# A two-layer convolution kernel: the 3x3 weights transformed in other rooms, their taps loaded first, image 0 on two queues, and new costs in the planner

## The chip, the core and the metric

The kernel runs on one core of a Trainium2 chip. Five engines matter here. TensorE (PE in the profile) multiplies matrices, and its weight loads have a row of their own (PEld). VectorE (DVE) and ScalarE (ACT) do elementwise work. GpSimd (POOL) and SyncE (SP) mostly issue transfers; ScalarE can issue them too. Each engine runs its own instructions strictly in the order of the program and waits for the others on semaphores. All transfers run on the core's 16 DMA engines, whatever engine issued them. The metric is the time of one execution on the device in microseconds. Three runs of the kernel before gave 2394.2, 2396.96 and 2401.03 us; the median, 2396.96 us, is the time before. The profiled execution spans 2394.4 us.

## The reference

Sixteen images of 1024 channels and 32x32 pixels, all float32, pass through two residual layers. Cut to what matters (`bn` is a scale and a shift per channel, `unfold3x3` gives the nine shifted copies of a map):

```python
# layer 0: bottleneck with 3x3 local self-attention, 32 heads of 8 channels
h    = relu(bn(conv1x1(x, w_conv1)))                # 1024 -> 256
q, k = relu(bn(conv1x1(h, wq))), relu(bn(conv1x1(h, wk)))
v    = bn(conv1x1(h, wv))
attn = softmax(einsum('bgdhw,bgdkhw->bgkhw', q, unfold3x3(k) + pos))   # over 9 taps
out  = einsum('bgdkhw,bgkhw->bgdhw', unfold3x3(v), attn)
x    = relu(bn(conv1x1(relu(bn(out)), w_conv3)) + x)                   # 256 -> 1024
# layer 1: bottleneck with an ordinary 3x3 convolution
h    = relu(bn(conv1x1(x, w1)))                     # 1024 -> 256
h    = relu(bn(conv3x3(h, w2)))
x    = relu(bn(conv1x1(h, w3)) + x)                 # 256 -> 1024
```

## The kernel before

The work is a hand-written list of stages per image. P is the first convolution of layer 0 (C) followed by the projections to k and q (Q) and to v (V). F is layer 0's last convolution fused with layer 1's first. W is the 3x3 convolution of four images at once, in Winograd form. U is layer 1's last convolution. The list begins `P0 P1 P2 P3 F0 P4 F1 ...` and ends `F12 F13 F14 U10:0123 F15 U10:4567 U11:01234 W12 U11:567 U12 U13 U14 U15`. TensorE walks it in this order.

VectorE does the attention (`logits`, `weighted`) and the Winograd transforms (`transform`, and `along`, `middle`, `last` in `winograd_conv`). ScalarE empties TensorE's accumulators (results, k, q, v, `by_offset`), seeds them with the residual input (L396), applies the exponentials (L642) and the relu of a finished attention (L704). Because each engine is in order, the place of every VectorE and ScalarE instruction among the others is fixed when the program is built. That is the task of class `Side`: a planner with two clocks of estimates, `tensor` and `vector`. A stage adds its cost to `tensor`; a job on VectorE yields the estimated cost of its next part, which is added to `vector`; a part is put into the program when its time on the `vector` clock comes within 4 us of `tensor`. An attention job starts no sooner than `RELAY` = 13 us after its operands were sent, and its exponentials are put into ScalarE's program when the `tensor` clock gets near the time planned for them. The estimates take no part when the kernel runs; they only set the order.

Before the first image the kernel must prepare weights. `load_taps` fetches the 3x3 weights (the taps, six transfers of 384 KB), `winograd_weights` transforms them: for each of two halves m, `sums` makes five rows along one axis, and `along` makes six rows (i) of the result from these, each 768 KB, which SyncE stores to DRAM as `uw` (L291, 12 stores). `sums` is three or four ScalarE and six VectorE instructions. Each row is built in a tile of pool `hpool` (5 buffers, shared with h, q and the attended maps), so a row can't begin before an earlier store has left its buffer. `load_scaled`, `scale_rows` and `scale_weights` scale two more weights and store them as `ws`. The planner runs both as `side.first` jobs from time 24 on. Pool `apool` holds the attention's operands under the tags qc, bnk, bnv, pc and e; at the start they are empty, except that the taps lie in e and bnv.

Attention of an image takes its q, k, v and position terms back from DRAM in another layout: they are stored (`q<-q`, `bnk<-kp`, `pos<-by_offset`) and loaded again (L575, `qc`, `bnk`, `pc`, `bnv`), which `relay` issues on GpSimd.

Transfers of image 0's input go out on ScalarE's queue, those of the others on GpSimd's (L345). `Side.held` and `release` hold the exponentials of image 0 back until the first convolution of image 2 has been emptied (L1066).

Of the kernel before, what the change touches and what calls it, by code (L numbers as in the profile page):

```python
# [72 lines left out]
def sa_bottleneck_kernel(ctx: ExitStack, tc: tile.TileContext, x, w1t, wqkvt, w3t, u1t, u2t, u3t, params, out):  # L73
# [92 lines left out]


    members = const.tile([P, G], F32, tag="members", name="members")
    nc.gpsimd.memset(members, 1.0)
    for base, sign in ((0, 1), (HEAD_DIM - 1, -1)):  # L170
        nc.gpsimd.affine_select(
            out=members,
            in_=members,
            compare_op=ALU.is_ge,
            fill=0.0,
            base=base,
            pattern=[[-sign * HEAD_DIM, G]],
            channel_multiplier=sign,
        )

# [20 lines left out]


    kp = const.tile([P, NW, H + 2, PW], F32, tag="kp", name="kp")
    nc.gpsimd.memset(kp, 0.0)
    vh = const.tile([P, NW * VROWS, VW], F32, tag="vh", name="vh")


# [23 lines left out]
    def scale_weights():  # L233

        for which in range(2):

            scale = scales[which].rearrange("p (m o) -> p o m", o=NC)
            shape = [P, NW, NC // 2, P]
            for half in range(2):
                t = scaled[which, half].rearrange("p n (o m) -> p n o m", m=P)  # L240
                nc.vector.tensor_tensor(
                    t, t, scale[:, half * NC // 2 :][:, : NC // 2].unsqueeze(1).to_broadcast(shape), ALU.mult
                )
                nc.sync.dma_start(ws[which, half], scaled[which, half])
                yield 1.3
# [14 lines left out]

    def winograd_weights():

        n = 3 * WID
        first, second = (ppool.tile([P, 4 * HW], F32, tag="t", name="g") for _ in range(2))
        one, two, three = first[:, : 2 * HW], first[:, 2 * HW :], second[:, : 2 * HW]

        def sums(dst, a, s, t0, t1):

            nc.scalar.activation(t0, a[1], AF.Identity, scale=-1 / 6)
            nc.scalar.activation(t1, a[1], AF.Identity, scale=1 / 12)  # L270
            nc.vector.tensor_add(s, a[0], a[2])
# [5 lines left out]
            nc.scalar.activation(dst[0], a[0], AF.Identity, scale=0.25)  # L277
            if dst[5] is not None:
                nc.scalar.activation(dst[5], a[2], AF.Identity)

        def along(m, i, row):

            t = hpool.tile([P, 2 * HW], F32, tag="h", name="u")[:, : NI * WID]
            u = t.rearrange("p (j o) -> p j o", j=NI)
            small = three[:, 2 * n :].rearrange("p (j o) -> p j o", o=WID)
            sums(
                [u[:, COLUMNS.index(j)] for j in range(NI)],
                [row[:, j * WID : (j + 1) * WID] for j in range(3)],
                small[:, 0], small[:, 1], one[:, 2 * n : 2 * n + WID],
            )  # L290
            nc.sync.dma_start(uw[i, :, :, m].rearrange("k p j o -> p k (j o)"), t.rearrange("p (k n) -> p k n", k=3))  # L291

        for m, g in enumerate(taps):
            rows_ = [one[:, :n], one[:, n : 2 * n], two[:, :n], two[:, n : 2 * n], three[:, :n]]

            s, t = three[:, n : 2 * n], second[:, 2 * HW :]
            sums(rows_ + [None], g, s, t[:, :n], t[:, n : 2 * n])
            yield 6.0
            for i, row in enumerate(rows_ + [g[2]]):
                along(m, i, row)  # L300
                yield 3.0

    def inside(t, n):
        return t[:, n, 1 : 1 + H, 1 : 1 + W]
# [10 lines left out]
    def more_loads():  # L315

        while loads and live[0] < CHUNKS + RESULTS - 1:
# [24 lines left out]
                t = xpool.tile([P, NK * 2 * PART], F32, tag="x", name=name)  # L342
                t = t if kind == "V" else t[:, :HW]

            (nc.scalar if kind == "x" and b == 0 else nc.gpsimd).dma_start(t, src)  # L345
            loaded[loads.pop(0)] = t
            live[0] += 1

# [110 lines left out]
    def project(b):  # L459
# [84 lines left out]
        side.add(b)  # L544
        written.add(("qk", b))
        relay("qk", b)
        yield 2.5
# [46 lines left out]
    def logits(b):  # L594
# [4 lines left out]
        for k in range(0, KK, 2):  # L599
            of = min(2, KK - k)  # L600
            for two in range(of):
                i, j = divmod(k + two, 3)
                nc.vector.tensor_tensor(  # L603
                    by_row(t[:, two]), by_row(qc), kc[:, :, i : i + JROWS, j : j + W], ALU.mult
                )
            yield 2.3 * of
            u = t[:, :of]
            nc.vector.tensor_add(u[:, :, 0:4], u[:, :, 0:4], u[:, :, 4:8])  # L608
            nc.vector.tensor_add(u[:, :, 0:2], u[:, :, 0:2], u[:, :, 2:4])
            nc.vector.tensor_add(e[:, k : k + of, :], u[:, :, 0], u[:, :, 1])  # L610
            yield 2.3 * of
# [8 lines left out]
        yield 3.5  # L620

        def tree(op, to):
            t = zpool.tile([P, 4, JPIX], F32, tag="z", name="tree")
# [100 lines left out]
    def transform(b, src):  # L724
# [28 lines left out]
        d = [AP(src.tensor, src.offset + i * VW, [src.ap[0], [4 * VW, LINES], [1, VW]]) for i in range(NI)]  # L753
        for make, two in pairs:
            make([t[:, i] for i in two], d)
            yield 3.4

        room = form_room(b)
        t = t.rearrange("p i l w -> p (i l) w")
        for make, two in pairs:  # L760
            v = [zpool.tile([P, HW], F32, tag="z", name="v")[:, : NI * PART] for _ in two]
            make([u.rearrange("p (l c) -> p l c", c=TR) for u in v], [t[:, :, at : at + TR] for at in PLACES])
            for j, u in zip(two, v):
                at = COLUMNS.index(j)
                nc.sync.dma_start(
                    room[:, at // 2, :, b % NK, at % 2].rearrange("i p e -> p i e"),
                    u.rearrange("p (i e) -> p i e", i=NI),
                )
            if two != (1, 2):
                key = b - b % NK, two == (0, 5)  # L770
                forms[key] = forms.get(key, 0) + 1
                more_loads()

            yield 4.3, 0.0 if b % NK == NK - 1 else 3.0

    def winograd_conv(b):

# [69 lines left out]
        def last(i):  # L847
# [11 lines left out]
            if i == 4:  # L859
# [4 lines left out]
                return 11.0  # L864
# [5 lines left out]
        for one, two in ROWS:  # L870
            for part in range(3):
                for i in (one, two):
# [3 lines left out]
                    elif part == 1:  # L876
                        copied(i, twos, 1.0)
                        side.other(along(i))
                        if i == 0:

                            middle(3, 0, 4.0)
                            side.other(6.0)
                    else:
                        side.other(last(i))
                    yield CHUNK + 0.3

    hidden_one = {}

# [8 lines left out]
    class Side:  # L897
# [3 lines left out]
        def __init__(self):  # L901
            self.tensor = self.vector = 8.0
            self.jobs, self.firsts, self.exp, self.ready = [], [], None, {}
            self.held = False

        def add(self, b):

# [6 lines left out]
        def begins(self):  # L914

            other, at = None, 1e6
            if self.jobs:
# [1 line left out]
                what = other["needs"], other["b"]  # L919
                at = max(self.vector, other["at"], come[what] + RELAY if what in come else 1e6)  # L920
                if self.exp:
                    at = 1e6 if self.held else max(at, self.exp[0] + EXP)
            if self.firsts:
                job = self.firsts[0]
                ready = max(self.vector, job["at"])
# [3 lines left out]

        def step(self):  # L930
            job, self.vector = self.begins()
            if self.exp and not self.held and ("needs" in job or self.exp[0] < self.tensor):
                self.fire()
            cost = next(job["parts"], "end")
            if cost == "end":
# [7 lines left out]
                job["needs"] = cost  # L943
            elif callable(cost):
                self.exp = self.vector - 0.0, cost
                if job["b"] == 0:

                    self.held = True
            else:
                self.vector += cost  # L950

# [3 lines left out]
            self.exp = None  # L955
            self.jobs[0]["at"] = max(at, self.tensor) + EXP

        def release(self):

            if self.held:  # L960
                self.held, at = False, self.exp[0]
                self.fire()
                self.jobs[0]["at"] = at + EXP

        def run(self):
            while True:
                if self.exp and not self.held and self.exp[0] < self.tensor + 4.0:
# [89 lines left out]
    def first_conv(b):  # L1057

        ps = two_sums()
        for c in range(NC):  # L1060
            reduce_part(c, ps, loaded.pop(("x", b, c)), "w1")
            free()
            if c == NC - 1:
                h = hidden[b] = hpool.tile([P, NW, HW], F32, tag="h", name=f"h_{b}")
                for n in range(NW):
                    nc.scalar.activation(  # L1066
                        h[:, n, :], ps[n], RELU, bias=col("L0_conv_bn1_b", n), scale=col("L0_conv_bn1_s", n)
                    )
# [358 lines left out]
```

## Time and profile before

| | value | where from |
|---|---|---|
| time, median of 3 | 2396.96 us | the times |
| span of the profiled execution | 2394.4 us | the page |
| PE busy | 2357.5 us, 98% | page, part 1 |
| DVE busy | 2163.4 us, 90% | page, part 1 |
| ACT busy | 933.2 us, 39% | page, part 1 |
| moved in the first 100 us | 370 GB/s, DMA share 1.00 | the table of windows |
| moved over the span | 289 GB/s | page, part 2 |

PE's busy share counts pipelined instructions, so 98% doesn't mean 98% of its peak; what it does say is that PE has only some 37 us without an instruction. The list of PE's waits tells what ended each of them. In the timeline a row gives the start, the length, the engine, the line, the operation, what it writes and reads, and in brackets the idle time ahead of it and what ended that. A row can stand for several instructions of the same kind (x8). For DMA issues the row tells when the queue's instruction ran, and the DMA view from when to when the bytes moved.

### The profile page before, as it was taken

The numbers are of one execution on the slowest core, as the hardware profiler recorded it, in microseconds if no ns is written. First come the engines' busy times: TensorE is split into PE (matmuls) and PEld (weight loads), VectorE is DVE, ScalarE is ACT, GpSimd is POOL, SyncE is SP. The second block draws the span as 40 slices with busy tenths as digits, with TensorE's granted clock in tenths as the row PEclk, the third lists the DMA queues.
The fourth block names the chain that finished last, engine by engine and source line by source line (L and its number), as shares of the span: only waits on it lengthen the run. The fifth ranks groups of instructions, "written<-read, shape, count | busy, mean of one in ns | idle before, by whom it ended". The sixth has DMA issues, their size and how long they took to land. (4 is left out here: it accounts for less than half of the span.)

```text
span 2394.4 us, 18854 instructions
## 1 busy us (share of the span) xinstructions
PE 2357.5 (98%) x6240; PEld 1141.1 (48%) x6240; DVE 2163.4 (90%) x1783; ACT 933.2 (39%) x891; POOL 490.8 (20%) x901
## 2 busy tenths in 40 slices
PE   8999999999999999999999999999999999999998
PEld 3443444444466444444466444444466444434843
DVE  4899999999999999998999999989989999874687
ACT  3324142323122574443122574334222553344278
POOL 3212121212121231111111232111111221111222
PEclk9999999999999999999999999999999999999999
DMA  9968696878797898676898997787798986787877
GB/s 362 362 215 307 251 301 211 276 284 265 273 341 264 318 393 301 233 266 227 250 315 293 302 404 294 240 283 276 239 323 299 316 332 224 252 281 266 328 285 293
DMA packets 296769, 691.08 MB, mean 289 GB/s; under 512 B 20832, under 2 KB 167264, under 8 KB 288224
## 3 DMA queue, kind: packets, MB, share of 16 engines
q0 software_dynamic: 119648, 470.88, 54.1%
q1 hardware_dynamic: 175648, 214.49, 27.9%
q10 hardware_dynamic: 1376, 4.51, 0.5%
q8 instruction: 50, 0.82, 0.1%
q14 instruction: 47, 0.39, 0.0%
HBM read 416.09 MB, written 273.70 MB: 288 GB/s over the span
## 5 line engine op out<-in xcount | busy, mean ns | idle before, releaser
L405 PE MATMUL ps<-a,w 128*128 128x512 f32 x1024 | 461.8, 596 | 6.6 <-ACT a L704 5.5
L373 PE MATMUL ps<-result,u 128*128 128x512 f32 x1024 | 457.8, 592 | 0.0
L373 PE MATMUL ps<-x,w 128*128 128x512 f32 x1024 | 444.4, 595 | 6.8 <-DMA x<-in_x_dram 6.8
L660 DVE TENSOR_TENSOR acc<-e,bnv 128x2048 f32<-128x2048 f32 x144 | 327.6, 2284 | 31.7 <-ACT e L642 28.6
L405 PE MATMUL ps<-y,u 128*128 128x512 f32 x768 | 331.3, 592 | 1.2 <-ACT ps L396 1.2
L603 DVE TENSOR_TENSOR prod<-qc,bnk 128x2048 f32<-128x2048 f32 x144 | 324.1, 2287 | 1.7
L432 ACT ACTIVATE result<-ps,par 128x1024 f32<-128x1024 f32 x128 | 142.5, 1113 | 457.9 <-PE ps L405 389.1
L405 PEld LDWEIGHTS ps<-a,w 128*128 128x128 f32 x1024 | 195.5, 191 | 255.2 <-issue 243.9
L373 PEld LDWEIGHTS ps<-x,w 128*128 128x128 f32 x1024 | 195.3, 191 | 252.5 <-issue 252.3
L373 PEld LDWEIGHTS ps<-result,u 128*128 128x128 f32 x1024 | 194.4, 190 | 245.1 <-issue 237.7
L678 DVE TENSOR_TENSOR acc<-acc 128x2048 f32<-128x2048 f32 x128 | 293.4, 2292 | 4.4
L405 PEld LDWEIGHTS ps<-y,u 128*128 128x128 f32 x768 | 145.8, 190 | 184.8 <-issue 180.8
L469 PE MATMUL ps<-h,wqk 128*128 128x512 f32 x512 | 222.3, 592 | 0.0
L433 POOL DMA_DIRECT2D r<-result x128 | 68.7, 537 | 632.1 <-ACT result L432 626.6
L608 DVE TENSOR_TENSOR prod<-prod 128x2048 f32<-128x2048 f32 (+1 forms) x80 | 166.2, 2078 | 2.5
L469 PEld LDWEIGHTS ps<-h,wqk 128*128 128x128 f32 x512 | 97.2, 190 | 122.6 <-issue 110.0
L1066 ACT ACTIVATE h<-ps,par 128x1024 f32<-128x1024 f32 x32 | 38.5, 1204 | 284.2 <-PE ps L373 284.2
L432 ACT ACTIVATE result<-ps,bn_sh 128x1024 f32<-128x1024 f32 x96 | 106.6, 1111 | 100.2 <-PE ps L405 98.4
L481 ACT ACTIVATE kp<-ps,par 128x1024 f32<-128x1024 f32 x64 | 77.4, 1210 | 154.9 <-PE ps L469 113.1
L396 ACT ACTIVATE ps<-s 128x1024 f32<-128x1024 f32 x128 | 131.2, 1025 | 2.5
L345 POOL DMA_DIRECT2D x<-in_x_dram x120 | 63.7, 532 | 291.3 <-PE ps L373 222.5
L469 PE MATMUL ps<-h,wv 128*128 128x512 f32 x256 | 117.0, 610 | 4.2 <-ACT by_offset L522 4.2
(376 smaller groups left out, 2618.1 us busy)
## 6 DMA issues: line engine op xcount, KB each, us to landing
s<-in_x_dram POOLq DMA_DIRECT2D x128, 512.0 KB, 6.2
r<-result POOLq DMA_DIRECT2D x128, 512.0 KB, 3.8
out_dram<-result POOLq DMA_DIRECT2D x126, 512.0 KB, 6.5
x<-in_x_dram POOLq DMA_DIRECT2D x120, 512.0 KB, 5.0
r<-r POOLq DMA_DIRECT2D x111, 512.0 KB, 7.2
v<-v SPq DMA_DIRECT2D x96, 408.0 KB, 4.5
U<-uw SPq DMA_DIRECT2D x72, 512.0 KB, 4.8
bnk<-kp SPq DMA_DIRECT2D x32, 680.0 KB, 7.0
```

What stands on the lines that cost most here:

```text
L345: (nc.scalar if kind == "x" and b == 0 else nc.gpsimd).dma_start(t, src)
L373: nc.tensor.matmul(ps[n][:, halves(half)], wt[:, c % (NC // 2), n * P : (n + 1) * P], src[:, halves(half)], start=(c == first), stop=(c == ...
L396: nc.scalar.activation(ps, loaded.pop((self.kind, self.b, o)), AF.Identity)
L405: nc.tensor.matmul(self.ahead[o][:, halves(half)], pieces[key][:, n, o % (NC // 2) * P :][:, :P], self.src[:, n, halves(half)], start=Fals ...
L432: nc.scalar.activation(to_, ps, RELU, bias=self.shift(o), scale=1.0)
L433: nc.gpsimd.dma_start(to, t)
L469: nc.tensor.matmul(ps[:, halves(half)], pieces[key][:, m, at : at + P], h[:, m, halves(half)], start=(m == 0), stop=(m == NW - 1),)
L481: nc.scalar.activation(dst, src, func, bias=col(f"L0_conv_{name}_b", n), scale=col(f"L0_conv_{name}_s", n),)
L603: nc.vector.tensor_tensor(by_row(t[:, two]), by_row(qc), kc[:, :, i : i + JROWS, j : j + W], ALU.mult)
L608: nc.vector.tensor_add(u[:, :, 0:4], u[:, :, 0:4], u[:, :, 4:8])
L660: nc.vector.tensor_tensor(by_row(dst), rows(e[:, k, :]).unsqueeze(1).to_broadcast([P, HEAD_DIM, JROWS, W]), vc[:, :, i : i + JROWS, j : j ...
L678: nc.vector.tensor_add(acc, acc, t)
```

## The change

It has four parts.

1. **Rooms.** A row of the transformed 3x3 weights is no longer built in `hpool` alone, but in tiles that the attention doesn't use yet (qc, bnk, e), in a free quarter of `second` (`four`), or in `hpool`. ScalarE's share of a row (`parts_of`) is split from VectorE's (`sums`) and is put one row ahead (`begin` before `finish`), with its own pair of scratch columns.
2. **Taps first, two queues.** The taps of the first half go out ahead of everything else on GpSimd, those of the second right after; the helper mask and the clearing of `kp` follow. Of image 0's eight input pieces four stay on ScalarE's queue and four go to SyncE's. The two loads for the scaled weights move to the third and fourth step of image 0.
3. **Costs.** The numbers that jobs yield to the planner are replaced by measured ones, and the two jobs of weights start at 15 instead of 24.
4. **No hold.** `held` and `release` go: image 0's exponentials are planned as the others' are.

All of it moves work; the arithmetic is the same.

```diff
@@ at_first
     def at_first():
+        load_taps(0)
+        more_weights()
         more_weights()
         more_loads()
+        load_taps(1)
+        head_members()
+        nc.gpsimd.memset(kp, 0.0)
         norms()
-        for m in range(NW):
-            load_taps(m)
-        load_scaled()
-        scale_rows()
-        for _ in range(3):
+        for _ in range(2):
             more_weights()
         position_table()
-        side.first(winograd_weights(), 24.0, 0.0)
-        side.first(scale_weights(), 24.0, 0.0)
+        side.first(winograd_weights(), 15.0, 0.0)
+        side.first(scale_weights(), 15.0, 0.0)
+        hooks["conv1", 0, 2] = load_scaled
+        hooks["conv1", 0, 3] = scale_rows
@@ winograd_weights
+        def room(where):
+
+            if where == "h":
+                t = hpool.tile([P, 2 * HW], F32, tag="h", name="u")
+            elif where == "four":
+                t = four
+            else:
+                shape = {"e": [P, KK, JPIX], "qc": [P, HEAD_DIM, JPIX], "bnk": [P, HEAD_DIM, HALO]}[where]
+                t = apool.tile(shape, F32, tag=where, name="u").rearrange("p a b -> p (a b)")
+            return t[:, : NI * WID]
+
+        rooms = (("qc", "bnk", "four", "h", "qc", "bnk"), ("h", "e", "qc", "four", "bnk", "e"))
...
-            for i, row in enumerate(rows_ + [g[2]]):
-                along(m, i, row)
-                yield 3.0
+            begun = begin(m, 0, rows_[0])
+            for i in range(NI):
+                following = begin(m, i + 1, (rows_ + [g[2]])[i + 1]) if i + 1 < NI else None
+                finish(m, i, *begun)
+                begun = following
+                yield 2.6
@@ more_loads
-            (nc.scalar if kind == "x" and b == 0 else nc.gpsimd).dma_start(t, src)
+            engine = nc.gpsimd
+            if kind == "x" and b == 0:
+                engine = nc.scalar if c < NC // 2 else nc.sync
+            engine.dma_start(t, src)
@@ logits
             nc.vector.tensor_add(e[:, k : k + of, :], u[:, :, 0], u[:, :, 1])
-            yield 2.3 * of
+            yield 4.24 if of == 2 else 2.36
@@ transform
             make([t[:, i] for i in two], d)
-            yield 3.4
+            yield 3.2
...
-            yield 4.3, 0.0 if b % NK == NK - 1 else 3.0
+            yield 4.05, 0.0 if b % NK == NK - 1 else 3.0
@@ Side
-                    at = 1e6 if self.held else max(at, self.exp[0] + EXP)
+                    at = max(at, self.exp[0] + EXP)
...
-                if job["b"] == 0:
-
-                    self.held = True
@@ first_conv
-                if b == 2:
-                    side.release()
```

Smaller costs change too: 2.3 to 2.29 per product in `logits`, 3.5 to 3.55 for the position terms, 2.5 to 1.1 after the positions in `project`, 1.3 to 2.0 in `scale_weights`, 11.0 to 11.4 and 6.0 to 5.5 in the 3x3 convolution, and its step of CHUNK + 0.3 becomes CHUNK (3.43).

More of the change, by code (lines that the diff above doesn't have):

```diff
@@ L168, in sa_bottleneck_kernel, with head_members @@
     members = const.tile([P, G], F32, tag="members", name="members")
[L169 to L179, printed above, removed]
+    def head_members():
+        nc.gpsimd.memset(members, 1.0)
+        for base, sign in ((0, 1), (HEAD_DIM - 1, -1)):
+            nc.gpsimd.affine_select(
+                out=members,
+                in_=members,
+                compare_op=ALU.is_ge,
+                fill=0.0,
+                base=base,
+                pattern=[[-sign * HEAD_DIM, G]],
+                channel_multiplier=sign,
+            )
     offsets = const.tile([P, NW, NPOS], F32, tag="offsets", name="offsets")
@@ L205, in sa_bottleneck_kernel @@
     kp = const.tile([P, NW, H + 2, PW], F32, tag="kp", name="kp")
-    nc.gpsimd.memset(kp, 0.0)
     vh = const.tile([P, NW * VROWS, VW], F32, tag="vh", name="vh")
@@ L244, in scale_weights @@
                 nc.sync.dma_start(ws[which, half], scaled[which, half])
-                yield 1.3
+                yield 2.0
     taps = []
@@ L264, in winograd_weights, with parts_of, sums @@
         first, second = (ppool.tile([P, 4 * HW], F32, tag="t", name="g") for _ in range(2))
-        one, two, three = first[:, : 2 * HW], first[:, 2 * HW :], second[:, : 2 * HW]
-        def sums(dst, a, s, t0, t1):
+        one, two, three, four = first[:, : 2 * HW], first[:, 2 * HW :], second[:, : 2 * HW], second[:, 2 * HW :]
+        def parts_of(a, t0, t1, to0, to5):
             nc.scalar.activation(t0, a[1], AF.Identity, scale=-1 / 6)
             nc.scalar.activation(t1, a[1], AF.Identity, scale=1 / 12)
+            nc.scalar.activation(to0, a[0], AF.Identity, scale=0.25)
+            if to5 is not None:
+                nc.scalar.activation(to5, a[2], AF.Identity)
+        def sums(dst, a, s, t0, t1):
             nc.vector.tensor_add(s, a[0], a[2])
@@ L276, in sums, with begin, finish @@
                 nc.vector.scalar_tensor_tensor(to, s, 1 / 6, t1, ALU.mult, op)
[L277 to L283, printed above, removed]
-            u = t.rearrange("p (j o) -> p j o", j=NI)
[L285 to L290, printed above, removed]
+        def room(where):
[8 more added lines that the diff above has]
+        rooms = (("qc", "bnk", "four", "h", "qc", "bnk"), ("h", "e", "qc", "four", "bnk", "e"))
+        small = [t[:, 2 * n :].rearrange("p (j o) -> p j o", o=WID) for t in (one, two, three)]
+        def begin(m, i, row):
+            t = room(rooms[m][i])
+            u = t.rearrange("p (j o) -> p j o", j=NI)
+            dst = [u[:, COLUMNS.index(j)] for j in range(NI)]
+            a = [row[:, j * WID : (j + 1) * WID] for j in range(3)]
+            t0, t1 = small[i % 2][:, 0], small[i % 2][:, 1]
+            parts_of(a, t0, t1, dst[0], dst[5])
+            return t, dst, a, t0, t1
+        def finish(m, i, t, dst, a, t0, t1):
+            sums(dst, a, small[2][:, 0], t0, t1)
             nc.sync.dma_start(uw[i, :, :, m].rearrange("k p j o -> p k (j o)"), t.rearrange("p (k n) -> p k n", k=3))
@@ L294, in winograd_weights @@
             rows_ = [one[:, :n], one[:, n : 2 * n], two[:, :n], two[:, n : 2 * n], three[:, :n]]
-            s, t = three[:, n : 2 * n], second[:, 2 * HW :]
-            sums(rows_ + [None], g, s, t[:, :n], t[:, n : 2 * n])
+            parts_of(g, four[:, :n], four[:, n : 2 * n], rows_[0], None)
+            sums(rows_ + [None], g, three[:, n : 2 * n], four[:, :n], four[:, n : 2 * n])
             yield 6.0
-            for i, row in enumerate(rows_ + [g[2]]):
-                along(m, i, row)
-                yield 3.0
+            begun = begin(m, 0, rows_[0])
[4 more added lines that the diff above has]
+                yield 2.6
     def inside(t, n):
@@ L546, in project @@
         relay("qk", b)
-        yield 2.5
+        yield 1.1
         for n, cost in enumerate(halo("bnv", 2, AF.Identity)):
@@ L605, in logits @@
                 )
-            yield 2.3 * of
+            yield 2.29 * of
             u = t[:, :of]
@@ L610, in logits @@
             nc.vector.tensor_add(e[:, k : k + of, :], u[:, :, 0], u[:, :, 1])
-            yield 2.3 * of
+            yield 4.24 if of == 2 else 2.36
         pc = projected[b]["pos"]
@@ L619, in logits @@
         nc.vector.tensor_tensor(part, part, pc[:, 2:4].unsqueeze(1).to_broadcast(shape), ALU.add)
-        yield 3.5
+        yield 3.55
         def tree(op, to):
@@ L863, in last @@
                 middle(4, 1, 8.0)
-                return 11.0
+                return 11.4
             r = 0 if i == 0 else 3
@@ L881, in winograd_conv @@
                             middle(3, 0, 4.0)
-                            side.other(6.0)
+                            side.other(5.5)
                     else:
                         side.other(last(i))
-                    yield CHUNK + 0.3
+                    yield CHUNK
     hidden_one = {}
@@ L903, in __init__ @@
             self.jobs, self.firsts, self.exp, self.ready = [], [], None, {}
-            self.held = False
         def add(self, b):
@@ L931, in step @@
             job, self.vector = self.begins()
-            if self.exp and not self.held and ("needs" in job or self.exp[0] < self.tensor):
+            if self.exp and ("needs" in job or self.exp[0] < self.tensor):
                 self.fire()
@@ L956, in fire @@
             self.jobs[0]["at"] = max(at, self.tensor) + EXP
[L958 to L963, printed above, removed]
         def run(self):
             while True:
-                if self.exp and not self.held and self.exp[0] < self.tensor + 4.0:
+                if self.exp and self.exp[0] < self.tensor + 4.0:
                     self.fire()
```

## The prediction

> **What bounds the kernel now.** I read the page first, part 1 with the header, for who could set the end:
>
> ```profile
> span 2394.4 us, 18854 instructions
> PE 2357.5 (98%) x6240; PEld 1141.1 (48%) x6240; DVE 2163.4 (90%) x1783; ACT 933.2 (39%) x891; POOL 490.8 (20%) x901
> ```
>
> TensorE does the same 6240 matmuls before and after, so the time is its matmul time plus its gaps: 2394.4 - 2357.5 = 36.9 us. The change can win only what it takes out of these gaps and out of matmuls made slow by them. The list of TensorE's waits names the larger ones (total, how often, longest):
>
> ```profile
> PE ps L373 <- DMA x<-in_x_dram: 6.8, 1, 6.8
> PE ps L405 <- ACT a L704: 5.5, 2, 3.5
> PE ps L469 <- ACT by_offset L522: 4.2, 1, 4.2
> PE ps L800 <- ACT z L823: 3.5, 3, 1.7
> PE ps L405 <- ACT ps L396: 2.3, 2, 1.2
> PE ps L800 <- DMA U<-uw: 2.2, 2, 2.0
> PE ps L1233 <- ACT result L432: 2.1, 1, 2.1
> PE ps L514 <- ACT q L481: 1.9, 1, 1.9
> ```
>
> The timeline of TensorE shows where they stand and what follows each. The bracket is the gap ahead of the row:
>
> ```profile
> 6.75 29.95 PE L373 MATMUL ps<-x,w 128*128 128x512 f32 x64 [6.75 <-DMA x<-in_x_dram]
> 53.35 1.09 PE L514 MATMUL ps<-q,pos 64*32 64x512 f32 x14 [1.95 <-ACT q L481]
> ...
> 2118.08 3.78 PE L405 MATMUL ps<-a,w 128*128 128x512 f32 x4 [3.47 <-ACT a L704]
> 2123.89 7.21 PE L405 MATMUL ps<-a,w 128*128 128x512 f32 x12 [2.03 <-ACT a L704]
> ...
> 2218.98 5.38 PE L800 MATMUL ps<-V__1_8303,U 128*128 128x256 f32 x16 [2.01 <-DMA U<-uw]
> ```
>
> Matmuls after a gap are long: four take 3.78 us at 2118, whereas eight take 3.70 us at 202. The table of windows has the granted clock, third from the end, for the stretches after the gaps in image 3 (by_offset) and image 15:
>
> ```profile
> 205.00:220.00 15.00, 10.82 (x19) 4.32 (x18) 14.79 (x9) 7.50 (x7) 3.98 (x7) 0.77 1.06 348
> 2114.00:2130.00 16.00, 10.50 (x16) 3.86 (x15) 12.25 (x14) 5.65 (x6) 1.60 (x3) 0.68 0.85 291
> ```
>
> So a gap costs itself and a tail of slow matmuls. Tails: by_offset (eight matmuls of V in 6.65 us instead of 3.70) 3.0; image 15, where 64 matmuls in 27.63 us elsewhere make 0.43 for one, (3.78 - 1.72) + (7.21 - 5.15) = 4.1; U<-uw, 5.38 - 3.62 = 1.8.
>
> The timeline of ScalarE tells why by_offset was late:
>
> ```profile
> 203.75 1.24 ACT L704 ACTIVATE a<-a,par 128x1024 f32<-128x1024 f32 x1 [4.67 <-DMA a<-a]
> 206.80 1.24 ACT L704 ACTIVATE a<-a,par 128x1024 f32<-128x1024 f32 x1 [1.81 <-DMA a<-a]
> 207.95 1.19 ACT L481 ACTIVATE kp<-ps,par 128x1024 f32<-128x1024 f32 x1
> 209.04 1.01 ACT L522 ACTIVATE by_offset<-ps 128x1024 f32<-128x1024 f32 x1
> ```
>
> ScalarE stood at the relu of image 0's attention, whose data VectorE had delivered too late; k's eviction and by_offset queued behind it, and TensorE behind those. Image 15 is the same wait, with a directly in TensorE's way. Both say VectorE is late; its first attention starts only at 92.03 us and then it runs almost without a gap to 2102.
>
> **What the Trainium skill says.** "TensorE: Matmul & The Clock Gate", section "What's actually happening": TensorE falls to half its clock after an idle window of about 3.4 us and recovers after a busy one of that length. The trace agrees on size: half speed follows the gaps of 4.18 and 3.47 us, and the window 48 to 56 us, with the gap of 1.95, has a granted clock of 1.00. "DMA: Bandwidth & Descriptors", section "Issuing engines are not separate DMA queues": queues of several engines run on the same 16 DMA engines and save only issue time. The trace agrees: DMA share 1.00 at 370 GB/s over the first 100 us, so new queues shift bytes, they add none. Same page, "Queues, rings and completion order": each DMA engine takes turns between the queues it has work for, and drains one queue in order. So a small store on SyncE's queue waits behind all that SyncE issued before; stores of uw took a median 11.9 us to land.
>
> **The change part by part.** The order of TensorE's instructions is identical in both kernels; that of ScalarE and VectorE differs.
>
> *Taps first, two queues.* In before, ScalarE issued eight pieces of x over 15.25 us and only then loaded its table; its first operation on taps ran at 17.95 us. With four pieces issue takes about 8 us, and the taps are ahead of everything on GpSimd, so the weights start about 8 us earlier, VectorE's work on them too. But 1.2 MB of taps now shares the engines with the first x: +0.7 us on the 6.75 us gap (from 0 where SyncE's queue is short, to 1.2 MB at 0.37 MB/us = 3.2).
>
> *Rooms.* In before VectorE waited 14.7 us (four times) for uw stores and ScalarE as long. In the new order ScalarE makes its part of all six rows of half 0 **before** it empties image 0's first convolution (h_0 at 35.0 us). Row 4 reuses qc, so it waits for store 1; row 5 reuses bnk and waits for store 2. SyncE has 5.5 MB ahead of the end of store 2. If the queues take equal turns, ScalarE's 2.15 MB are gone after about 16 us, then SyncE has half of 0.40 MB/us: 33 us; if GpSimd's larger transfers take more, 41. Behind row 5 wait h_0, behind h_0 TensorE's Q of image 0 and everything after. I take 39: wait 3.9 us, above the idle window, hence a tail of 3.0 (as after by_offset); bounds 0 and 10. In half 1, row 5 in e waits for store 8 ahead of image 0's by_offset, with 10.9 MB on SyncE's queue; I take +4, bounds 0 and 8. Sum for the opening: 0.7 + 3.9 + 3.0 + 4 = **+11.6**. The old gap of 1.95 at image 0's q goes (its cause, two rows waiting for uw at 51.48, moves): -1.95.
>
> *No hold, new costs.* Work of VectorE per image is unchanged (49.2 us of logits, 46.0 of weighted sums); it is only reordered, attention ahead of transforms. VectorE's idle 28.6 us (7 waits) for exponentials should shrink, since ScalarE now has most of them 7 to 60 us earlier among its instructions. Image 0's k comes back (relay of bnk) after about 28.4 MB in all, which before took until 78 us (28.87 MB in the first 80), so logits start at 82 to 87 instead of 92. VectorE is then 5 to 10 us earlier and TensorE, through the opening, about 10 later: image 0's relu finds its data, though it now stands two evictions earlier. Gap and tail at 210: 4.18 + 3.05 = **-7.2**. VectorE needs to be only 5.5 us earlier against TensorE at image 15: 5.5 + 4.1 = **-9.6**. For the third convolution of image 12 one v-store block is issued earlier, so U<-uw may come in time; I count the gap, -1.9, and leave its tail as reserve. Waits for z: jobs are placed by truer durations; 3.5 us to about 2, **-1.5**, bounds 0 and -3.5.
>
> Scaled weights loaded later, the mask and the clearing of kp later: hidden, as GpSimd is busy 25% of the first 100 us and the scaled weights are first needed at the first F, after 210 us.
>
> Sum: 11.6 - 1.95 - 7.2 - 9.6 - 1.9 - 1.5 = -10.6, so 2396.96 - 10.6 = **2386**.
>
> **The rivals.**
> - *Clean opening.* Store 2 lands by 35 us and store 8 before it matters. For: SyncE's half share gives 33 us, and VectorE's rows start 8 us earlier. Against: the share of 1.00 leaves no slack. The 11.6 falls away, but then TensorE is not delayed and image 0's relu, standing two evictions earlier, makes it slip about 5 once: -10.6 - 11.6 + 5 = -17, **2380**.
> - *Gains eaten.* Stores land late (41 us and more): the opening costs 20 instead of 11.6, and half of the -1.9 and -1.5 stays out: -10.6 + 8.4 + 1.7 = -0.5, **2396**. For: uw stores already took 11.9 us to land. Against: both waits at their late bound.
> - *Slower.* The opening costs 24, and the wait at image 15 stays because VectorE meets other late exponentials (-9.6 lost): -10.6 + 12.4 + 9.6 = +11.4, **2408**. For: VectorE is 90% busy and all order has moved. Against: 28.6 us of waits are there to be shortened.
>
> **How the numbers follow.** Forecast 2386: 0.5; clean opening 0.2; eaten 0.17; slower 0.13. The range 2374 to 2400 adds to the clean opening its further bounds (tail 1.8, z 2.0, and some of ps and result) and takes in the eaten case; it leaves out the slower one and little else. Faster by over 0.3% is below 2389.8, slower above 2404.2. The first two cases give 0.7, of which 0.08 lies above 2389.8, as the forecast's margin is 4 us: faster 0.62, same 0.25, slower 0.13.
>
> **What would show it.** The list of TensorE's waits after: by_offset's 4.2, a's 5.5 and q's 1.9 gone, and a new wait on h L1066 or on uw near 37 us with half clock behind it. ScalarE's timeline: rows 4 and 5 waiting for uw ahead of h_0. VectorE's first logits at 82 to 87 us. The forecast is wrong if image 0's convolution is emptied at 35 us (then clean), if the wait for a at image 15 is still there, or if a new wait appears in the middle, where I counted none.

## The result, and the profile after

The changed kernel is **slower**, by 0.74%: 2415.66 us (median of 4 runs, 2411.57 to 2421.06) against 2397.08, a ratio of 1.0074 with an interval of 1.0054 to 1.0095. The forecast was 2386 us, and its range ended at 2400.

The page of the changed kernel, header and part 1:

```profile
span 2412.1 us, 18855 instructions
PE 2360.9 (98%) x6240; PEld 1143.0 (47%) x6240; DVE 2165.6 (90%) x1783; ACT 931.9 (39%) x891; POOL 491.0 (20%) x901
```

The busy time of the engines hardly moved. TensorE's idle time is now 2412.1 - 2360.9 = 51.2 us instead of 36.9, and its busy time grew by 3.4, for matmuls are slow after some of the gaps. Its list of waits (total, times, longest), in the same form as before:

```profile
PE ps L401 <- ACT result L460: 12.0, 4, 4.6
PE ps L401 <- DMA x<-in_x_dram: 8.7, 2, 6.4
PE ps L828 <- ACT z L851: 6.7, 1, 6.7
PE ps L497 <- ACT h L1083: 5.1, 1, 5.1
PE ps L828 <- issue: 3.1, 2, 2.3
PE ps L433 <- ACT a L732: 2.3, 1, 2.3
PE ps L1248 <- ACT result L460: 2.1, 1, 2.1
PE ps L828 <- DMA V__2_8376<-v: 1.7, 1, 1.7
PE ps L828 <- DMA U<-uw: 0.9, 1, 0.9
```

The waits that the forecast removed are gone or smaller: by_offset (4.2), q (1.9), a (5.5, now 2.3). New are those for `result` (L460, the output of layer 0's last convolution, which layer 1's first needs), a second one for x, and a longer one for z. The one for h is the one that the forecast expected near 37 us.

Both kernels give TensorE the same 6240 matmuls in the same order. So one can pair them by number and read how much later the changed kernel starts each. That lateness, worked out from the two traces, tells where the time went (a minus means that the changed kernel is ahead):

| stretch of the kernel before, us | lateness at its end | step | forecast |
|---|---|---|---|
| opening, to 60 | +4.2 | +4.2 | +11.6 - 1.95 = +9.7 |
| by_offset of image 3, at 210 | -3.2 | -7.4 | -7.2 |
| F at 328 | +3.1 | +6.3 | 0 |
| 690 to 840 | -1.6 | -4.7 | -1.5 (all z) |
| 1100 to 1250 | +13.1 | +14.7 | 0 |
| 1250 to 2110 | +24.6 | +11.5 | 0 |
| attended map of image 15, at 2118 | +19.1 | -5.4 | -9.6 |
| U<-uw, at 2219 | +16.4 | -2.8 | -1.9 |
| end | +17.7 | +1.3 | 0 |

At 220 us the changed kernel is 3.2 us ahead. **It loses everything in the middle**, where the change moved nothing but the order of the instructions on the engines other than TensorE.

The opening in the timeline of ScalarE after:

```profile
25.89 0.42 ACT L272 ACTIVATE g<-g 128x256 f32<-128x256 f32 x1 [0.91 <-DVE g L284]
37.41 0.42 ACT L273 ACTIVATE u<-g 128x256 f32<-128x256 f32 x1 [11.10 <-DMA uw<-u]
...
39.80 0.42 ACT L273 ACTIVATE u<-g 128x256 f32<-128x256 f32 x1 [1.06 <-DMA uw<-u]
40.12 0.40 ACT L275 ACTIVATE u<-g 128x256 f32<-128x256 f32 x1
40.43 2.28 ACT L1083 ACTIVATE h<-ps,par 128x1024 f32<-128x1024 f32 x2
```

Rows 4 and 5 wait for stores of uw (11.10 and 1.06 us), h_0 is emptied behind them at 40.43 instead of 35.02, and TensorE waits 5.07 us. VectorE's first row of logits after:

```profile
85.70 4.50 DVE L631 TENSOR_TENSOR prod<-qc,bnk 128x2048 f32<-128x2048 f32 x2 [10.94 <-DMA bnk<-bnk]
```

It starts at 85.70, 6.3 us earlier than before, and still waits for k's way back.

Now one link of the loss in the middle, in order of time. VectorE, image 8:

```profile
1012.50 2.28 DVE L708 TENSOR_TENSOR acc<-acc,se 128x2048 f32<-128x2048 f32 x1
1025.99 4.49 DVE L631 TENSOR_TENSOR prod<-qc,bnk 128x2048 f32<-128x2048 f32 x2 [11.21 <-DMA a<-acc]
```

Pool `ppool` has two buffers. A transform was begun between two parts of image 7's weighted sum and isn't finished, so it holds one; the sum (`acc`) holds the other until its store has landed. The products of image 8 must wait 11.21 us for that store. In the kernel before, a transform is begun inside the same sum as well, at 989.96 us, and image 8's products still follow the sum at once:

```profile
1019.21 1.01 DVE L729 SCALAR_TENSOR_TENSOR v<-form,v 128x816 f32<-128x816 f32 x1
...
1024.78 2.29 DVE L680 TENSOR_TENSOR acc<-acc,se 128x2048 f32<-128x2048 f32 x1
1026.99 4.49 DVE L603 TENSOR_TENSOR prod<-qc,bnk 128x2048 f32<-128x2048 f32 x2
```

The difference is which job ends first. Before, the sum had two more parts to go, so the transform made its last use of `form` at 1019.21, ahead of the end of the sum, and gave its buffer back in time. In the changed kernel the sum ends first, and the transform's last four instructions on `form` stand behind the products of image 8. The kernel before does wait for stores of sums (8.7 us in all), but only ahead of transforms.

Then ScalarE, whose exponentials of image 8 stand ahead of an eviction of `result`:

```profile
1098.29 1.06 ACT L670 ACTIVATE e<-e 128x1024 f32<-128x1024 f32 x1 [10.17 <-DVE e L663]
1099.68 1.27 ACT L670 ACTIVATE e<-e 128x1280 f32<-128x1280 f32 x1 [0.34 <-DVE e L663]
1100.86 1.10 ACT L460 ACTIVATE result<-ps,par 128x1024 f32<-128x1024 f32 x1
```

GpSimd, whose relay of the next v stands ahead of loads of x:

```profile
1191.25 0.59 POOL L603 DMA_DIRECT2D bnv<-bnv  x1 [15.01 <-DVE acc L688]
1191.83 1.60 POOL L373 DMA_DIRECT2D x<-in_x_dram  x3
```

And ScalarE again, where z has to wait for a buffer that image 9's maximum tree still uses, with TensorE behind it:

```profile
1241.65 1.94 ACT L851 ACTIVATE z<-ps 128x1024 f32<-128x1024 f32 x2 [11.47 <-DVE mx L654]
```

```profile
1198.46 7.97 PE L401 MATMUL ps<-x,w 128*128 128x512 f32 x14 [2.27 <-DMA x<-in_x_dram]
...
1242.73 5.83 PE L828 MATMUL ps<-V__1_4508,U 128*128 128x256 f32 x16 [6.70 <-ACT z L851]
```

Three times, on ScalarE, GpSimd and ScalarE again, an instruction that TensorE needs stands behind one, or is itself one, that waits for a late VectorE. TensorE pays 2.42 us at 1102, 2.27 at 1198 and 6.70 at 1243, and slow matmuls after the last two.

### The profile page after: what moved, and what is told of

Its sections match the earlier page's. It is cut to its first block, busy times and chain, and to the rows that moved or that the text cites. A ratio compares the mean times of both kernels' runs of the same rounds, so it can differ in the third digit from the quotient of the medians.

```text
span 2412.1 us, 18855 instructions
## 1 busy us (share of the span) xinstructions
PE 2360.9 (98%) x6240; PEld 1143.0 (47%) x6240; DVE 2165.6 (90%) x1783; ACT 931.9 (39%) x891; POOL 491.0 (20%) x901
## 5 line engine op out<-in xcount | busy, mean ns | idle before, releaser
L401 PE MATMUL ps<-result,u 128*128 128x512 f32 x1024 | 463.5, 598 | 12.0 <-ACT result L460 12.0
L688 DVE TENSOR_TENSOR acc<-e,bnv 128x2048 f32<-128x2048 f32 x144 | 327.6, 2284 | 24.1 <-ACT e L670 21.1
L460 ACT ACTIVATE result<-ps,par 128x1024 f32<-128x1024 f32 x128 | 142.4, 1113 | 458.6 <-PE ps L433 399.3
L460 ACT ACTIVATE result<-ps,bn_sh 128x1024 f32<-128x1024 f32 x96 | 106.6, 1112 | 105.6 <-PE ps L433 101.5
L851 ACT ACTIVATE z<-ps 128x1024 f32<-128x1024 f32 x48 | 49.1, 1024 | 184.9 <-PE ps L828 136.8
```

Of the source, the lines that this page charges most:

```text
L401: nc.tensor.matmul(ps[n][:, halves(half)], wt[:, c % (NC // 2), n * P : (n + 1) * P], src[:, halves(half)], start=(c == first), stop=(c == ...
L460: nc.scalar.activation(to_, ps, RELU, bias=self.shift(o), scale=1.0)
L688: nc.vector.tensor_tensor(by_row(dst), rows(e[:, k, :]).unsqueeze(1).to_broadcast([P, HEAD_DIM, JROWS, W]), vc[:, :, i : i + JROWS, j : j ...
```

## The experiments

The planner's two clocks have a value when the first logits of an image are put into the program. Taking (real start - planned time) on VectorE, less the same for TensorE's next matmul, gives **how late VectorE is against the order it was given**, in us (e4 and e13 are explained below):

| image | before | changed | e4 | e13 |
|---|---|---|---|---|
| 0 | 12.0 | 11.1 | 4.0 | 5.5 |
| 1 | 12.1 | 9.1 | 2.0 | 4.8 |
| 7 | -3.4 | -1.6 | -3.4 | -2.7 |
| 8 | -7.0 | 9.2 | -4.1 | -1.5 |
| 12 | -10.5 | -2.7 | 6.3 | -0.8 |

Two errors stand out: the plan starts image 0's attention 11 to 12 us too early (in both kernels), and the changed one has a jump at image 8. A third suspect is the new costs: the old ones, a little too high, give the plan slack. All ratios below are to the kernel before on the same chip, with their intervals.

**e1: old costs for the jobs.**

```diff
-            yield 2.29 * of
+            yield 2.3 * of
...
-            yield 4.24 if of == 2 else 2.36
+            yield 2.3 * of
...
-                    yield CHUNK
+                    yield CHUNK + 0.3
```

In the same way the positions go back to 2.5, their terms to 3.5, the transform to 3.4 and 4.3, and the 3x3 convolution to 11.0 and 6.0. The costs of the two jobs on weights stay new.

> The changed kernel (rooms, taps first, two queues, start at 15, no hold) with the old costs for everything after the weights: logits (2.3 per product, 2.3 per tap for the sums, 3.5, 2.5 after the positions), transforms (3.4, 4.3) and the 3x3 convolution (11.0, 6.0, CHUNK + 0.3). Theory 'costs without slack' (the measured durations leave VectorE's real waits out, so ScalarE's instructions are placed for a VectorE that is earlier than the real one, and new waits come up from image 2 on): most of the loss goes, 2383 to 2397. Theory 'start of the plan' (logits of image 0 are planned at 66 instead of 77 us, the real ones start only 6 us earlier, and the error is handed on): 2408 to 2418, as the start is still at 15.

Measured 2400.71 us, 1.0014 (1.0008 to 1.0021). That lies between the two bands, nearer to that of the costs. VectorE meets the same store at image 8, 6.98 us, and TensorE has no gap over 0.3 us between 840 and 1250 us: here the plan takes it up. The late start it doesn't take up: ScalarE stands 6.06 us at the exponentials of image 1, and TensorE waits 6.77 us behind them at 233.

**e2: the new costs alone.** Edit: the same lines, the other way, in the kernel before, and with them the new costs of the two jobs on weights.

> The kernel before with all new costs and nothing else: rooms, taps, queues, start at 24 and hold are the old ones. 'Costs without slack': 2405 to 2422. 'Start of the plan': logits of image 0 are planned at 77 as before, so 2393 to 2401.

Measured 2404.23 us, 1.0037 (1.0023 to 1.0050). They cost half of what the whole change costs, and just less than expected. TensorE waits 4.50 us for a `result` at 333, close to the changed kernel's wait at 329, and 4.37 for a at 487, but has no gap over 0.3 us from there to 1617. VectorE is 11.3 and 6.4 us late at images 1 and 2 here, though image 0's logits are planned at 75 us, nearly as before; so the tighter costs alone can bring a wait there.

**e3: the hold back.** Edit: `held` and `release` as in the kernel before, in the changed one.

> The changed kernel with the hold of image 0's exponentials back; the planned times of all other work are the same, only image 0's exponentials move behind the first convolution of image 2. 'Costs without slack' and 'start of the plan' both: 2412 to 2418, no effect, since the time is lost from 329 us on. A third theory, 'the hold' (ScalarE in front of image 0's exponentials delays what is behind it): down to 2400 or less.

Measured 2427.21 us, 1.0130 (1.0112 to 1.0149): a miss for all theories. With the hold, image 0's exponentials come later, and so does VectorE (20.3 us late at image 1, against 9.1); GpSimd stands at a relay that waits for it, ahead of loads of x:

```profile
187.68 0.56 POOL L603 DMA_DIRECT2D bnv<-bnv  x1 [19.26 <-DVE acc L688]
188.23 1.05 POOL L373 DMA_DIRECT2D x<-in_x_dram  x2
```

TensorE waits 11.3 us for x at 196. So dropping the hold was right with this opening.

**e14: the hold alone.** Edit: `held` and `release` taken out of the kernel before.

> The kernel before without the hold of image 0's exponentials, all else as before. Planned times are those of before. 'Each change of order is a new draw of collisions': anything from 2390 to 2405. If the hold did its work in the old opening: 2399 to 2410.

Measured 2395.36 us, 1.0004 (0.9996 to 1.0011): nothing. A new wait of 6.1 us (h behind image 0's exponentials) takes the place of the 4.2 us for by_offset and what followed it.

**e4: image 0 planned later.**

```diff
-                come[what, b] = max(side.vector, side.tensor) if b else side.tensor
+                come[what, b] = max(side.vector, side.tensor) if b else side.tensor + 11.0
```

> The changed kernel with the arrival of image 0's operands entered 11 us later in the plan, the lateness that VectorE's first logits show against the planned time and TensorE. 'Start of the plan': the wait at 329 us (5.4 us with its tail) and most others go, 2395 to 2402. 'Costs without slack': the first wait may go, the later ones at 1102, 1198 and 1243 stay, 2405 to 2416.

Measured 2401.25 us, 1.0017 (1.0007 to 1.0026). That is the band of the plan's start. As the table shows, VectorE's lateness at images 0 and 1 falls to 4 and 2 us, and of the wait at 329 only 0.8 us is left. A new wait of 7.0 us for z comes at 698. The jump has not gone: it has moved to image 12. There VectorE waits 8.64 us for the store of image 11's sum, and TensorE 7.1 us at 1629.

**e5: both.** Edit: e1 and e4 together.

> Both cures together: the changed kernel with the old costs of all jobs after the weights and image 0's operands entered 11 us later. If the two errors (no slack in the costs, a plan that starts too early) cost time in different places, the gains add: 2415.7 - 15 - 14 = 2387, 2382 to 2392. If each alone already cures the same waits: 2397 to 2402, no better than one.

Measured 2406.43 us, 1.0035 (1.0022 to 1.0048): worse than either. No theory of additive parts holds. VectorE's lateness has neither of the two errors at full size (6.0 and 5.4 us at images 0 and 1, -2.9 and 0.2 at 8 and 12), but the order is drawn anew, and TensorE is held up twice by a late z (9.1 us at 701, 7.1 at 1793).

**e6, e7: rows 4 and 5 in hpool.**

```diff
-        rooms = (("qc", "bnk", "four", "h", "qc", "bnk"), ...
+        rooms = (("qc", "bnk", "four", "h", "h", "h"), ...
```

> The changed kernel with rows 4 and 5 of half 0 in hpool instead of qc and bnk, so that ScalarE needn't wait for two stores of uw ahead of h_0; costs and plan as changed. 'The opening's wait is paid': the 5.1 us and their 2 us of slow matmuls go, 2406 to 2411. 'It is eaten': VectorE is 11 us late to TensorE in the first images anyway, so TensorE waits later what it doesn't wait here: 2413 to 2418.

> Old job costs, image 0 entered 11 us later, and rows 4 and 5 of half 0 in hpool. If the opening's wait is paid: 7 us below e5, 2378 to 2383. If it is eaten because VectorE's start then is later against TensorE: within 2 us of e5 or above it.

Measured 2419.44 us, 1.0090 (1.0074 to 1.0106), against 1.0074 for the changed kernel, and 2405.32, 1.0028 (1.0016 to 1.0041), against 1.0035 for e5. Both lie in the bands of "eaten", but not for its reason. In e6 h_0 no longer waits; TensorE waits 2.9 us for q and 2.6 for by_offset of image 0 instead, the latter behind another store of uw, and at 100 us its matmuls are 6.1 us late against the kernel before, where those of the changed kernel are 4.2 late. The edit moved the wait within the opening, so what a shorter opening would bring was not measured.

**e8: which costs.** Edit: e4 with the old costs of logits and positions only.

> The changed kernel with image 0 entered 11 us later and the old costs of the attention alone (logits and the 2.5 after the positions); transforms and 3x3 convolution keep the new ones. If the attention's slack (about 1.4 us per image) is what counts: near e5, 2384 to 2392. If it is the slack of the convolution's steps (0.3 us for each of its steps): near e4, 2398 to 2404.

Measured 2399.26 us, 1.0008 (0.9998 to 1.0017), in the second band: the attention's slack is not what counts, and with e5 nor is the rest of it once image 0 is planned later. Again image 12 waits for a store (8.64 us), and TensorE 7.5 us at 1622. The wait for z near 698 of e4 and e5 isn't there.

**e9, e10, e11: an unused tile.** `from_ppool` takes a tile of `ppool`; e9 adds one to the changed kernel, e10 to e8 and e11 to e4.

```diff
+        if b == 8:  # e10 and e11: where a transform's tile came between
+            from_ppool([P, 4 * HW], F32, tag="t", name="spare")
```

> The changed kernel with one unused tile of ppool taken ahead of the products of image 8, nothing else. ppool has two buffers; in the changed order a transform's tile is taken between the attended sum of image 7 and the products of image 8, so the products land in the sum's buffer and VectorE waits 11.2 us for the sum's store. The unused tile takes that place. Theory 'one wait, handed on' (these 11 us are what makes TensorE wait at 1102, 1198 and 1243, together 15.4 us with slow matmuls): 2398 to 2404. Rival 'lateness from elsewhere' (the later waits come of the tight costs whatever image 8 does): 2410 to 2416.

> e8 (image 0 entered 11 us later, old costs of the attention) with an unused tile of ppool wherever a transform's tile was taken between one image's sum and the next image's products (images 8, 9 and 12). In e8 VectorE waits 8.6 us for a store at image 12, and TensorE 7.5 us at 1624 with 2 us of slow matmuls. If handed on the same way: 2399 - 10 = 2389, 2385 to 2392, below both kernels. If not: 2396 to 2401.

> e4 (all new costs, image 0 entered 11 us later) with the unused tile at images 8, 9 and 12. 'One wait, handed on': VectorE's 8.6 us at 1572 and TensorE's 7.1 us at 1629 with its 2.3 us of slow matmuls go, 2401 - 9.5 = 2392, 2388 to 2395. 'Lateness from elsewhere': 2399 to 2403.

Measured 2415.60 us, 1.0074 (1.0058 to 1.0091); 2398.90, 1.0014 (1.0005 to 1.0023); 2400.98, 1.0019 (1.0011 to 1.0026). All three lie in the bands of the rivals, but these decide nothing, for the wait was still there (8.6 us in e10 and e11), as VectorE's timeline of e9 shows:

```profile
1026.57 4.49 DVE L639 TENSOR_TENSOR prod<-qc,bnk 128x2048 f32<-128x2048 f32 x2 [11.39 <-DMA a<-acc]
```

A tile that nobody uses gives no buffer free: of two buffers one holds a transform in work, the other the sum.

**e12: the transform after the sum.**

```diff
-            if self.firsts:
+            whole = other and other["b"] == 7 and other["needs"] == "v"
+            if self.firsts and not whole:
```

> The changed kernel with no transform let in between the parts of image 7's weighted sum; it follows that sum whole. The times at which the plan fires the exponentials are those of the changed kernel for all images. So VectorE's 11.2 us at image 8 (the products wait for the store of image 7's sum, whose buffer they need) have a transform beside them. 'One wait, handed on': TensorE's waits at 1102, 1198 and 1243 (15.4 us with slow matmuls) go, 2398 to 2405. 'Lateness from elsewhere' (tight costs, whatever image 8 does): 2410 to 2416.

Measured 2408.78 us, 1.0056 (1.0044 to 1.0068), between the two bands. VectorE's products of image 8 now start without a wait:

```profile
1010.37 4.49 DVE L631 TENSOR_TENSOR prod<-qc,bnk 128x2048 f32<-128x2048 f32 x2
1014.77 1.00 DVE L767 TENSOR_TENSOR v<-form 128x816 f32<-128x816 f32 x1
```

Paired by matmuls, the step at 1102 goes whole (2.7 us), that at 1198 too (4.2), and of the one at 1243 not quite half, 3.4 us. So the chain from one store is shown for two of the three waits and for part of the third: 10.3 of 14.7 us. Later waits give 3.4 of these back, and the spans of the two traces differ by 7.5. By the ratios it is 0.18%, 4 us, and the two intervals overlap, so the times alone don't fix its size. What is left: 329, 1243 (3.8), 1641 to 1955.

**e13, e15: both errors out.** Edit: e12's, with image 11 for 7, in e8 (e13) and in e4 (e15).

> e8 (image 0 entered 11 us later, old costs of the attention) with no transform between the parts of image 11's weighted sum. In e8 VectorE waits 8.6 us for the store of that sum and TensorE 7.5 us at 1624 with 2.3 us of slow matmuls. 'One wait, handed on': 2399 - 10 = 2389, 2386 to 2392. 'Lateness from elsewhere': 2396 to 2400.

> e4 (all new costs, image 0 entered 11 us later) with no transform between the parts of image 11's weighted sum. 'One wait, handed on': TensorE's 7.1 us at 1629 and 2.3 us of slow matmuls go, 2401 - 9.5 = 2392, 2388 to 2395. 'Lateness from elsewhere': 2399 to 2403.

Measured 2390.09 us, 0.9983 (0.9973 to 0.9992), and 2391.46, 0.9987 (0.9978 to 0.9995). Both lie in the bands of "one wait, handed on". By the ratios the edit gives 6.0 us in e8 and 7.2 in e4, less than the 10 expected, by the medians 9.2 and 9.8. Both are **faster than the two kernels compared here**, if by less than 0.2% against the kernel before. TensorE's list of waits in e13:

```profile
PE ps L401 <- DMA x<-in_x_dram: 7.3, 1, 7.3
PE ps L828 <- ACT z L851: 4.7, 3, 1.8
PE ps L497 <- ACT h L1084: 4.0, 1, 4.0
...
PE ps L401 <- ACT result L460: 1.0, 1, 1.0
```

The 12.0 us for `result` are 1.0, and no single wait for z is above 1.8. In e15 the one of 7.1 us at 698 is still there, as in e4. e15 has **all** the new costs of the change. So the new costs are not bad in themselves: with image 0 planned 11 us later and one transform moved, they make a kernel that is faster than before. Over all runs, VectorE's products wait once for a sum's store (6 to 11 us) in every kernel except before, e12, e13, e14 and e15. Of those with the wait all are slower than the kernel before, e8 just within the noise; of those without it only e12 is, which keeps the early start.

## Why the prediction was wrong

The step that failed is the part on "No hold, new costs". It credited what a reordered VectorE and ScalarE would save at waits seen in the trace of before, and put new waits at none: "or if a new wait appears in the middle, where I counted none". There the runs show +6.3, +14.7 and +11.5 us, less 4.7, so +27.8 where -1.5 stood.

- **Opening: right in kind, too dear.** Rows 4 and 5 did wait ahead of h_0; they were released at 37.41 and 39.80 (I had taken 39). With the slow matmuls it came to 7.0 us of lateness where 0.7 + 3.9 + 3.0 = 7.6 stood; the gap itself was 5.1 instead of 3.9, and x came 0.3 us earlier instead of 0.7 later. The +4 for half 1 did not come, and the gap at q went with 2.8 instead of 1.95.
- **by_offset: right.** -7.4 against -7.2; the relu ahead of it now stands earlier and waits 0.86 us for its data. Logits at 85.70 lie in the forecast 82 to 87.
- **Image 15 and U<-uw: right in direction.** -5.4 for -9.6, since a's second wait went, but 2.3 us of the first stayed; -2.8 for -1.9.
- **"VectorE's idle 28.6 us for exponentials should shrink": it did, to 21.1, and no gain of TensorE's in the middle followed.** The exponentials stand earlier among ScalarE's instructions. That saves VectorE's time where it keeps to the plan, and costs ScalarE's where VectorE is late: at 1098 ScalarE stood 10.17 us. The prediction read one side of this trade only.
- **The rival on the slower side** had the right sign at 2408, for reasons that failed: the opening cost 4, not 24, and image 15's gain came. It named "all order has moved" without a figure.

What stands in place of the failed step: the change of order carries two weak points. With image 0 planned too early, VectorE is 7 to 11 us behind its places at images 0 to 2, until TensorE waits for it at 329 (e4 takes that wait away). The early start is not the only way to it, as e2 shows. And a wait that the plan doesn't know, for the store of a sum, throws VectorE back by 11 us at image 8, where it has no reserve. The kernel before starts as late, but is 7.0 us ahead of its plan at image 8, and its transform has given its buffer back when the sum ends. Taking the image 8 wait away shortens the stretch from 1100 to 1250 by 10.3 us in the traces (e12); planning image 0 later and taking the wait, then at image 12, away gives 0.87% (1.0074 to 0.9987, e15), more than the whole loss.

What stays open: how the rest of the loss splits. e1 shows that the old costs absorb the second weak point but not the first, e5 that they can meet new waits of their own; the costs' share can't be given as one number, as each edit redraws which stores and trees meet. The waits from 1652 to 1967 in the changed kernel (11.5 us with slow matmuls) were not taken away by themselves, and the wait for z near 700 us, which came with the later start in e4, e5, e7 and e15, was not followed up. The rooms, the taps and the earlier start of the weights were never run one by one.

## What to carry to other kernels

When a change alters estimates that only decide the order, the gain is not just the waits that the old trace shows: each in-order queue gets new neighbours, so look in the new order for what stands ahead of each instruction that the bottleneck engine needs, and which buffer it takes. A plan made of busy times alone carries no reserve, so enter the waits in it (here the arrival of the first operands, 11 us: 1.0074 to 1.0017). Loose costs are no sure cure: they helped in e1 and not in e5. With two buffers and two interleaved jobs, a tile of the other job must have been given back before this job's last tile waits for its store; the kernel before does so, the changed one doesn't.

## What was not expected of the hardware

The prediction took a gap of 3.4 us as what it needs for half clock, from the Trainium skill, "TensorE: Matmul & The Clock Gate", section "What's actually happening", and found the trace of before in agreement. The gap of 2.01 us at 2219, whose tail it priced at 1.8, already spoke against that. Shorter gaps do it as well, but not always. The table of windows, first of before, then of the changed kernel, granted clock third from the end:

```profile
2216.00:2226.00 10.00, 7.99 (x30) 6.45 (x29) 0.55 (x1) 2.05 (x2) 3.15 (x6) 0.83 0.93 317
...
1100.00:1108.00 8.00, 5.99 (x14) 2.77 (x15) 7.83 (x11) 5.05 (x5) 2.65 (x5) 1.00 0.52 171
1198.00:1206.00 8.00, 7.54 (x14) 3.33 (x15) 7.86 (x5) 0.00 (x0) 0.53 (x1) 0.79 1.01 357
1199.40:1202.50 3.10, 3.10 (x5) 1.35 (x4) 3.03 (x3) 0.00 (x0) 0.00 (x0) 0.50 1.02 341
```

After a gap of 2.42 us at 1102 the clock stays at 1.00, after one of 2.27 at 1198 it is 0.79, with 0.50 in the midst of that stretch. A tail after a gap of some 2 us is thus a chance, not a sure price. Its size is steadier, by an estimate that takes the clock as either 0.50 or 1.00: (1 - 0.79) x 8 / 0.5 = 3.4 us at half clock after the gap of 2.27, (1 - 0.83) x 10 / 0.5 = 3.4 after that of 2.01, and (1 - 0.77) x 15 / 0.5 = 6.9, twice as much, after before's gap of 4.18 at 210.

A store was long under way on a busy queue. SyncE's timeline of the changed kernel has the first two stores of uw from 20.57 us on, issued behind weights:

```profile
18.67 0.47 SPq L131 DMA_DIRECT2D wv<-in_wqkvt_dram  x1
20.57 3.00 SPq L313 DMA_DIRECT2D uw<-u  x2
```

ScalarE's row 4, which waits for the first of them, begins at 37.41, some 17 us after the issue; the median of such a store in the kernel before was 11.9 us.
